# Softmax sums over the partitions in four 128x32 tiles of the array instead of 64x64 tiles, in three of four groups of an attention

## The chip, the cores and the metric

The kernel runs on one core of a Trainium2 chip, in f32 throughout. The metric is the device time of one launch in microseconds. All runs quoted were fast, at a granted TensorE clock of 0.992 to 0.995.

## The reference, cut to what matters

A group norm, a 1x1 convolution and two bottlenecks are run over 8 images of 512 channels and 32x32 positions. Each bottleneck has a 3x3 convolution and an attention of four heads of 64 channels over 1024 positions:

```python
        qkv = conv2d(x, qkv_w, 0).reshape(b, 3, HEADS, HD, hw)
        q, k, v = (qkv[:, 0], qkv[:, 1], qkv[:, 2])
        r = (rw + rh).reshape(1, HEADS, HD, hw)
        logits = jnp.einsum('bhdi,bhdj->bhij', q, k + r) * HD ** (-0.5)
        a = jax.nn.softmax(logits, axis=-1)
        out = jnp.einsum('bhij,bhdj->bhdi', a, v)
```

The change touches only how the denominators of the softmax are summed.

## The kernel before

An attention is run in four groups: a pair of heads (`c`) and a half of the 1024 queries (`half`). Keys lie on the partitions. TensorE makes the logits of 128 keys at a time, ScalarE takes exponentials into `pt`, VectorE adds these over the key blocks into `acc` (128 partitions x 2 heads x 512 queries), and TensorE multiplies `pt` with V. What is then left of the denominator is a sum over the 128 partitions of `acc`:

```python
            def sums(g):
                ps = ps_big.tile([P, 2, HALF], F32, tag="big", name="s_ps")
                acc = accs.pop(g)
                for kh in range(2):
                    r = slice(kh * HD, (kh + 1) * HD)
                    for hd in range(2):
                        nc.tensor.matmul(
                            ps[hd * HD : (hd + 1) * HD, kh, :], ones[r], acc[r, hd, :],
                            start=True, stop=True,
                        )
                s_dram = tc.dram_tile([2, 2, HALF], F32, name=f"s_dram{at + g}")
                rows = [act.tile([P, HALF], F32, tag=t, name="s_row", bufs=2) for t in ("h", "t")]
                for kh, row in enumerate(rows):
                    nc.scalar.copy(row, ps[:, kh, :])
                    for hd in range(2):
                        nc.sync.dma_start(s_dram[kh, hd : hd + 1, :], row[hd * HD : hd * HD + 1, :])
                return ps, rows, s_dram
```

The sums of both halves of the partitions go to memory, come back spread over the partitions, are added (`total`), inverted, written and read once more, copied to 64 partitions for each head (`spread`). Then VectorE scales the output with them (`scale`). The main loop places these steps:

```python
            for i in range(len(pairs) + 1):
                if i < len(pairs):
                    added = logits(pairs[i])
                    g, at_q = divmod(i, NQ)
                    with tc.issue_after(added.ins):
                        if at_q == NQ - 2 and g > 0:
                            rss[g - 1] = spread(g - 1, s_drams[g - 1])
                        if at_q == 0 and g > 1:
                            scale(g - 2, rss.pop(g - 2))
                if i > 0:
                    times_v(pairs[i - 1])     # the last pair of a group also empties av: ScalarE copy, VectorE add
                    g, j0 = pairs[i - 1][0]
                    if j0 == 0:
                        if g > 0:
                            s_drams[g - 1] = sums(g - 1)[2]
                        ...                   # work of other stages behind this group
```

The last group's sums stay in PSUM on all partitions and are inverted there; the change leaves that group as it was. `ps_av`, the accumulator for V, has one buffer, so the next group's product with V waits until VectorE has emptied it.

Of the kernel before, what the change touches and what calls it, by code (L numbers as in the profile page):

```python
# [40 lines left out]
F32 = mybir.dt.float32  # L41
# [7 lines left out]
P = 128  # L49
# [8 lines left out]
def kernel(  # L58
# [16 lines left out]
    nc = tc.nc  # L75
# [8 lines left out]
    HALF = 512  # L84
# [9 lines left out]
    act = fast.enter_context(tc.tile_pool(name="act", bufs=1))  # L94
# [77 lines left out]
    ones = const.tile([P, HD], F32, name="ones")  # L172
# [64 lines left out]
    QP = 2 * HALF // P  # L237
    sums_all = const.tile([P, NSUM, QP], F32, name="sums_all")
# [8 lines left out]
    def stages(act, small, ps_big, ps_av, n_pt):  # L247
# [207 lines left out]
        def attention_fast(n, z, at, behind):  # L455
# [5 lines left out]
            ao = act.tile([P, NM, HW], F32, tag="z", name="ao")  # L461
# [4 lines left out]
            pts, accs, avs = {}, {}, {}  # L466

            def logits(pair):
                g, j0 = pair[0]
                c, half = groups[g]  # L470
                pt = act.tile([P, PAIR, 2, HALF], F32, tag="pt", name="pt", bufs=n_pt)
                pts[pair[0]] = pt
                for i, (_, j) in enumerate(pair):
                    ps = ps_big.tile([P, 2, HALF], F32, tag="big", name="l_ps")
                    for hd in range(2):
                        r = slice(hd * HD, (hd + 1) * HD)
                        for kh in range(2):
                            o = j * P + kh * HD
                            nc.tensor.matmul(  # L479
                                ps[kh * HD : (kh + 1) * HD, hd, :], kr[r, c, o : o + HD],  # L480
                                q[r, c, ts(half, HALF)], start=True, stop=True,
                            )
                    exp = nc.scalar.activation(pt[:, i], ps, AF.Exp, scale=SCALE)  # L483
                if pair is pairs[-1]:
                    with tc.issue_after(exp.ins):
                        table_of(AF.Silu)
                if j0 == 0:
                    accs[g] = act.tile([P, 2, HALF], F32, tag="acc", name="acc", bufs=2)
                    return nc.vector.tensor_tensor(accs[g], pt[:, 0], pt[:, 1], ALU.add)  # L489
                for i in range(PAIR):  # L490
                    ins = nc.vector.tensor_tensor(accs[g], accs[g], pt[:, i], ALU.add)  # L491
                return ins

            def times_v(pair):
                g, j0 = pair[0]
                c, half = groups[g]
                pt = pts.pop(pair[0])
                if j0 == 0:
                    avs[g] = ps_av.tile([P, 2, HALF], F32, tag="av", name="av_ps")
                for i, (_, j) in enumerate(pair):  # L500
# [3 lines that stand above are left out]
                            o = c * P + hd * HD  # L504
                            nc.tensor.matmul(  # L505
                                avs[g][hd * HD : (hd + 1) * HD, kh, :], vT[r, j, o : o + HD],
                                pt[r, i, hd, :], start=(j == 0), stop=(j == NJ - 1),
                            )
                if j0 + PAIR == NJ:
                    av = avs.pop(g)  # L510
                    dst = ao[:, c, ts(half, HALF)]
                    nc.scalar.copy(dst, av[:, 0])
                    nc.vector.tensor_tensor(dst, av[:, 1], dst, ALU.add)  # L513

            def sums(g):

                ps = ps_big.tile([P, 2, HALF], F32, tag="big", name="s_ps")
                acc = accs.pop(g)
                for kh in range(2):
# [11 lines that stand above are left out]
                        nc.sync.dma_start(s_dram[kh, hd : hd + 1, :], row[hd * HD : hd * HD + 1, :])  # L531
                return ps, rows, s_dram

            def total(g, s_dram):

                cs = small.tile([P, 2, QP], F32, tag="cs", name="cs", bufs=2)
                nc.sync.dma_start(cs, s_dram.rearrange("k h (i r) -> (h i) k r", r=QP))
                nc.vector.tensor_tensor(sums_all[:, at + g, :], cs[:, 0], cs[:, 1], ALU.add)
                return sums_all[:, at + g, :]

            def spread(g, s_dram):

                rs = act.tile([P, HALF], F32, tag="rs", name="rs", bufs=2)
                rc = small.tile([P, QP], F32, tag="rc", name="rc", bufs=2)
                nc.vector.reciprocal(rc, total(g, s_dram))
                r_dram = tc.dram_tile([2, HALF], F32, name=f"r_dram{at + g}")
                nc.sync.dma_start(r_dram.rearrange("h (i r) -> (h i) r", r=QP), rc)
                for hd in range(2):
                    nc.sync.dma_start(
                        rs[hd * HD : (hd + 1) * HD, :], r_dram[hd : hd + 1, :].to_broadcast([HD, HALF])  # L550
                    )
                return rs

            def scale(g, rs):
                c, half = groups[g]
                dst = ao[:, c, ts(half, HALF)]
                nc.vector.tensor_tensor(dst, dst, rs, ALU.mult)
# [5 lines left out]
            s_drams, rss = {}, {}  # L563
# [10 lines that stand above are left out]
                    times_v(pairs[i - 1])  # L574
                    g, j0 = pairs[i - 1][0]
                    if j0 == 0:
                        if g > 0:
                            s_drams[g - 1] = sums(g - 1)[2]
                        with tc.issue_after(added.ins):
                            behind.get(g, lambda: None)()  # L580
            with tc.issue_after(added.ins):
                behind.get(len(groups), lambda: None)()

            g = len(groups) - 1
            ps, rows, s_dram = sums(g)
            with tc.issue_after(added.ins):
                behind.get(len(groups) + 1, lambda: None)()
            scale(g - 1, rss.pop(g - 1))
# [1 line left out]
            nc.vector.tensor_tensor(rs, ps[:, 1, :], rows[0], ALU.add)  # L590
            nc.vector.reciprocal(rs, rs)
            scale(g, rs)
            return ao, lambda: total(g, s_dram)

        def attention_general(n, z):
            IB = 256
# [169 lines left out]
    ps_big = fast.enter_context(tc.tile_pool(name="ps_big", bufs=3, space=PSUM))  # L766
# [34 lines left out]
    for b in range(B):  # L801
# [54 lines left out]
        ao, check = s.attention_fast(0, z, b * N * NM * NH, {**{g: ahead for g in range(NG)}, NG: first, NG + 1: second})  # L856
# [28 lines left out]
        ao, check = s.attention_fast(1, z, (b * N + 1) * NM * NH, {1: ahead, NG: first, NG + 1: second})  # L885
# [26 lines left out]
    with tc.If(held < P):  # L912
        with ExitStack() as gs:
# [6 lines left out]
            g = stages(g_act, g_small, g_big, g_av, 3)  # L920
            with tc.For_i(0, B, 1) as b:
# [6 lines left out]
                for n in range(N):  # L928
                    z = g.conv3x3(n, g.tiles_in(yi), lambda oc: [load_u(n, oc, i) for i in range(PAIRS)])
                    ao = g.attention_general(n, z)  # L930
# [57 lines left out]
```

## Time and profile before

| | before |
|---|---|
| median of 3 runs | 2502.18 us (2498.42 to 2503.01) |
| span of the profiled run | 2497.3 us |
| TensorE, VectorE, ScalarE busy | 97%, 60%, 39% |
| TensorE's share of the chain that ended last | 86% |

The profile's chain of waits starts at the last instruction and goes back to what released each one. A microsecond taken from an instruction on it shortens the run, until another path is the longest. Time off it costs nothing. The lines are in the prediction.

### The profile page before, as it was taken

How to read it: one execution, taken by the hardware profiler on the slowest of the kernel's cores; microseconds unless marked ns; L12 is line 12 of the kernel's file. 1: busy time of each engine (PE TensorE's matmuls, PEld its weight loads, DVE VectorE, ACT ScalarE, POOL GpSimd, SP SyncE). 2: the span in 40 equal slices, each digit the busy share in tenths (PEclk: the TensorE clock that was granted, in tenths of full speed). 3: DMA queues.
4: the chain of work that ended last, by engine and by line, in shares of the span. 5: the costliest groups of instructions: out<-in, count | busy, mean ns of one | idle time of the engine just before them, and what ended most of it. 6: DMA issues, size and time to landing. Idle time of an engine off the chain costs nothing.

```text
span 2497.3 us, 35914 instructions
## 1 busy us (share of the span) xinstructions
PE 2424.1 (97%) x14626; PEld 1208.3 (48%) x14626; DVE 1497.6 (60%) x2530; ACT 969.9 (39%) x1328; POOL 104.6 (4%) x355
## 2 busy tenths in 40 slices
PE   6789999999999999999999999999999999999998
PEld 4436446363463634636355363644536454363543
DVE  7678554766456664666546665566564665636654
ACT  2453522525135261443514434153441534326252
POOL 1000000000100001000010000100001000010001
PEclk9899999999999999999999999999999999999999
DMA  6124014040140402304032040402205021050202
GB/s 234 61 91 154 27 39 169 15 152 11 57 150 15 152 15 73 130 15 152 15 119 89 19 143 15 173 35 64 98 14 202 10 74 55 18 194 11 72 10 65
DMA packets 88348, 200.42 MB, mean 80 GB/s; under 512 B 34032, under 2 KB 43760, under 8 KB 75888
## 3 DMA queue, kind: packets, MB, share of 16 engines
q1 hardware_dynamic: 74224, 152.40, 17.7%
q0 software_dynamic: 11808, 45.62, 5.1%
q8 instruction: 117, 1.92, 0.3%
q14 instruction: 55, 0.45, 0.1%
q10 hardware_dynamic: 2144, 0.03, 0.0%
HBM read 167.94 MB, written 30.08 MB: 79 GB/s over the span
## 4 chain that ended last, share of the span: by engine, by line
PE 86%; DVE 5%; ACT 3%; issue 2%; DMA 1%; SPq 0%; ACTq 0%; DVEq 0%
PE ps L266 34%; PE av_ps L505 15%; PE l_ps L479 14%; PE c_ps L673 13%; PE v_ps L445 4%; PE m_ps L694 4%; ACT pt L483 2%; PE s_ps L522 2%; DVE ao L513 1%; DVE acc L489 1%; DMA rs<-r_dram 1%; ACT t L252 1%; DVE acc L491 1%; DMA r_dram<-rc 0%; DVE v_in L325 0%
## 5 line engine op out<-in xcount | busy, mean ns | idle before, releaser
L483 ACT ACTIVATE pt<-l_ps 128x1024 f32<-128x1024 f32 x512 | 495.5, 1025 | 195.6 <-PE l_ps L479 195.6
L491 DVE TENSOR_TENSOR acc<-acc,pt 128x1024 f32<-128x1024 f32 x384 | 469.0, 1221 | 128.3 <-ACT pt L483 102.8
L505 PE MATMUL av_ps<-pt,vT 64*64 64x512 f32 x4096 | 485.4, 591 | 16.6 <-DVE ao L513 14.4
L479 PE MATMUL l_ps<-q,kr 64*64 64x512 f32 x4096 | 485.7, 592 | 7.3 <-ACT pt L483 7.3
L673 PEld LDWEIGHTS c_ps<-v_in,u 128*128 128x128 f32 x2688 | 302.6, 192 | 11.2 <-issue 6.7
L673 PE MATMUL c_ps<-v_in,u 128*128 128x128 f32 x2688 | 303.2, 275 | 4.0 <-DVE v_in L325 4.0
L505 PEld LDWEIGHTS av_ps<-pt,vT 64*64 64x64 f32 x4096 | 152.8, 133 | 312.6 <-issue 221.6
L479 PEld LDWEIGHTS l_ps<-q,kr 64*64 64x64 f32 x4096 | 153.4, 133 | 287.1 <-issue 263.4
L266 PE MATMUL ps<-z,qkv_sb 128*128 128x512 f32 x512 | 229.3, 595 | 0.4
L266 PE MATMUL ps<-x,w 128*128 128x512 f32 x512 | 227.4, 601 | 2.2 <-DVE x L401 2.2
L266 PE MATMUL ps<-ypad,w 128*128 128x512 f32 x512 | 227.8, 594 | 0.5 <-ACT t L252 0.5
L266 PEld LDWEIGHTS ps<-x,w 128*128 128x128 f32 x512 | 97.0, 192 | 130.5 <-issue 124.6
L489 DVE TENSOR_TENSOR acc<-pt 128x1024 f32<-128x1024 f32 x64 | 78.4, 1225 | 135.5 <-ACT pt L483 135.5
L266 PEld LDWEIGHTS ps<-ypad,w 128*128 128x128 f32 x512 | 96.5, 190 | 126.0 <-issue 124.6
L433 DVE TENSOR_TENSOR kr<-ps,rw_sb 128x512 f32<-128x512 f32 x64 | 41.2, 686 | 186.0 <-PE ps L266 186.0
L252 ACT ACTIVATE t<-ps,bh,sh 128x512 f32<-128x512 f32 x58 | 42.7, 775 | 274.6 <-PE ps L266 168.0
L266 PEld LDWEIGHTS ps<-z,qkv_sb 128*128 128x128 f32 x512 | 94.7, 190 | 107.2 <-issue 91.8
L756 DVE TENSOR_TENSOR t<-t,x_res 128x512 f32<-128x512 f32 x64 | 44.0, 692 | 170.2 <-ACT t L252 141.9
L529 ACT COPY s_row<-s_ps 128x512 f32<-128x512 f32 x128 | 68.7, 589 | 152.0 <-PE s_ps L522 152.0
L266 PE MATMUL ps<-y,w 128*128 128x512 f32 x256 | 118.0, 599 | 3.7 <-ACT t L252 3.7
L332 ACT COPY m<-c_ps 128x256 f32<-128x256 f32 x96 | 35.5, 369 | 220.8 <-PE c_ps L673 214.6
L266 PE MATMUL ps<-ylast,w 128*128 128x512 f32 x256 | 117.2, 595 | 0.0
(118 smaller groups left out, 2102.1 us busy)
## 6 DMA issues: line engine op xcount, KB each, us to landing
u<-u SPq DMA_DIRECT2D x84, 1024.0 KB
w<-in_cv_w_dram SPq DMA_DIRECT2D x25, 1024.0 KB
x<-in_x_dram SPq DMA_DIRECT2D x32, 512.0 KB
x_res<-in_x_dram POOLq DMA_DIRECT2D x64, 256.0 KB, 3.7
out_dram<-t POOLq DMA_DIRECT2D x62, 256.0 KB, 2.7
u<-u_new POOLq DMA_DIRECT2D x12, 1024.0 KB, 5.4
rs<-r_dram SPq DMA_DIRECT2D x96, 128.0 KB
raw<-in_m_cv_w_dram SPq DMA_DIRECT2D x8, 576.0 KB
```

The costliest lines, as they stand in the source:

```text
L252: return nc.scalar.activation(dst, src, AF.Silu, scale=sh[:, k : k + 1], bias=bh[:, k : k + 1])
L266: nc.tensor.matmul(ps[:, half, :], w_of(k), rhs_of(k, half), start=(k == begin), stop=(k == end))
L445: nc.tensor.matmul(ps[:, at, :], z[:, k, ts(j0 + at, P)], qkv_sb[:, n, k, 2 * C : 3 * C], start=(k == 0), stop=(k == NM - 1),)
L479: nc.tensor.matmul(ps[kh * HD : (kh + 1) * HD, hd, :], kr[r, c, o : o + HD], q[r, c, ts(half, HALF)], start=True, stop=True,)
L483: exp = nc.scalar.activation(pt[:, i], ps, AF.Exp, scale=SCALE)
L489: return nc.vector.tensor_tensor(accs[g], pt[:, 0], pt[:, 1], ALU.add)
L491: ins = nc.vector.tensor_tensor(accs[g], accs[g], pt[:, i], ALU.add)
L505: nc.tensor.matmul(avs[g][hd * HD : (hd + 1) * HD, kh, :], vT[r, j, o : o + HD], pt[r, i, hd, :], start=(j == 0), stop=(j == NJ - 1),)
L522: nc.tensor.matmul(ps[hd * HD : (hd + 1) * HD, kh, :], ones[r], acc[r, hd, :], start=True, stop=True,)
L529: nc.scalar.copy(row, ps[:, kh, :])
L673: nc.tensor.matmul(ps[:, row, col, :], us[i][:, k, row, col, :], vs[i][:, k, row, col, :], start=(k == 0), stop=(k == NM - 1),)
L694: nc.tensor.matmul(pss[oc][:, half, :], m2_sb[:, n, k, ts(oc, P)], ao[:, k, ts(half, HALF)], start=(k == 0), stop=(k == NM - 1),)
```

## The change

The intent: 128x32 tiles sum over all 128 partitions at once, one tile for each head and half of the group's queries. So each instruction has 256 columns, not 512, and there is no second half to add. The way in which TensorE's array is split, here into four tiles of 64x64 or four of 128x32, is called its mode below; the logits and the products with V stay in 64x64 tiles. ScalarE copies one 128x256 tile, one transfer takes four rows away, and the way back lands where the reciprocal reads.

```diff
             def sums(g):
+                NQ4 = HALF // 2
+                ps = ps_big.tile([P, NQ4], F32, tag="big", name="s_ps")
+                acc = accs.pop(g)
+                for at_q in range(4):
+                    hd, part = divmod(at_q, 2)
+                    nc.tensor.matmul(
+                        ps[at_q * 32 : (at_q + 1) * 32, :], ones[:, 0:32], acc[:, hd, ts(part, NQ4)],
+                        start=True, stop=True, tile_position=(0, at_q * 32),
+                    )
+                s_dram = tc.dram_tile([4, NQ4], F32, name=f"s_dram{at + g}")
+                row = act.tile([P, NQ4], F32, tag="h", name="s_row", bufs=2)
+                nc.scalar.copy(row, ps)
+                nc.sync.dma_start(s_dram, row[0:P:32, :])
+                return s_dram
+
+            def last_sums(g):
... (the sums as before, for the last group)
-            def total(g, s_dram):
-
+            def last_total(g, s_dram):
                 cs = small.tile([P, 2, QP], F32, tag="cs", name="cs", bufs=2)
                 nc.sync.dma_start(cs, s_dram.rearrange("k h (i r) -> (h i) k r", r=QP))
                 nc.vector.tensor_tensor(sums_all[:, at + g, :], cs[:, 0], cs[:, 1], ALU.add)
+
+            def total(g, s_dram):
+
+                nc.sync.dma_start(sums_all[:, at + g, :], s_dram.rearrange("a (i r) -> (a i) r", r=QP))
                 return sums_all[:, at + g, :]
... (the calls renamed)
```

More of the change, by code (lines that the diff above doesn't have):

```diff
@@ L577, in attention_fast @@
                         if g > 0:
-                            s_drams[g - 1] = sums(g - 1)[2]
+                            s_drams[g - 1] = sums(g - 1)
                         with tc.issue_after(added.ins):
@@ L584, in attention_fast @@
             g = len(groups) - 1
-            ps, rows, s_dram = sums(g)
+            ps, rows, s_dram = last_sums(g)
             with tc.issue_after(added.ins):
@@ L592, in attention_fast @@
             scale(g, rs)
-            return ao, lambda: total(g, s_dram)
+            return ao, lambda: last_total(g, s_dram)
         def attention_general(n, z):
```

## The prediction

> **What bounds the kernel now.** I read the page first: the busy shares, then its chain that ended last, then the costliest groups.
>
> ```profile
> PE 2424.1 (97%) x14626; PEld 1208.3 (48%) x14626; DVE 1497.6 (60%) x2530; ACT 969.9 (39%) x1328; POOL 104.6 (4%) x355
> ...
> PE 86%; DVE 5%; ACT 3%; issue 2%; DMA 1%; SPq 0%; ACTq 0%; DVEq 0%
> ...
> L529 ACT COPY s_row<-s_ps 128x512 f32<-128x512 f32 x128 | 68.7, 589 | 152.0 <-PE s_ps L522 152.0
> ...
> L332 ACT COPY m<-c_ps 128x256 f32<-128x256 f32 x96 | 35.5, 369 | 220.8 <-PE c_ps L673 214.6
> ```
>
> TensorE is the bound: it is busy 97% of the span, and 86% of the chain of work that ended last lies on it. VectorE (60%) and ScalarE (39%) have slack on average, so work taken from them counts only at the places where the chain passes through them. The ScalarE copies of the sums' rows, L529, run 128 times, twice for each of the 64 groups (8 images x 2 bottlenecks x 4 groups).
>
> Next I went through the whole chain, stretch by stretch. The piece of the sums (s_ps) is on it 62 times out of 64: 44 times at 0.86 us and twice at 0.90 us in the groups that the change touches, and 16 times at 1.02 us in each attention's last group, which it doesn't touch. So 46 of the 48 changed groups have their sums on the path, and TensorE time gained or lost there counts nearly in full. This stretch of the chain has two group boundaries of one attention (columns: start us, duration us, what, count):
>
> ```profile
> 897.86 1.72 PE av_ps L505 x16
> 899.58 0.90 PE l_ps L479 x8
> 900.48 0.02 issue
> 900.50 1.95 ACT pt L483 x2
> ...
> 904.22 0.70 DVE ao L513
> 904.91 0.04 issue
> 904.96 1.95 PE av_ps L505 x16
> 906.90 0.90 PE s_ps L522 x8
> ...
> 908.31 0.59 ACT s_row L529
> 908.90 0.94 ACT pt L483
> ...
> 912.86 2.25 DMA r_dram<-rc
> ...
> 915.62 3.98 DMA rs<-r_dram
> ```
>
> The first boundary is the usual kind: TensorE's next product with V waits until VectorE has emptied its one accumulator (L513), which stands behind the group's first two exponentials. The wait is short: logits start at 899.58, three stages of 1.72 us would end at 904.74, and the product starts at 904.96. The second is the rarer kind: the sums' copies delay the exponentials, these the adds, and then the reciprocal's way through memory ends last. DMA pieces "rs" stand only four times on the whole chain.
>
> **What the Trainium skill says.** Three places bear on this.
> - "TensorEngine Tiling (Array Packing)", Key Properties: "Changing tiling mode (not just tile) drains the TensorE". The trace agrees and gives the price, because this kernel changes between 64x64 tiles and the whole array elsewhere. The first line here is undisturbed, from another attention, the others are a stretch with changes:
>
> ```profile
> 727.46 6.87 PE ps L266 x16
> ...
> 932.43 7.06 PE ps L266 x16
> 939.49 1.02 PE s_ps L522 x8
> 940.51 3.63 PE ps L266 x8
> ```
>
>  Sixteen whole-array matmuls take 6.87 us, but 7.06 us right after tiled ones: 0.19 us for the change. The sums take 1.02 us in place of 0.86 when whole-array matmuls precede them: 0.16 us for a change the other way. After the small group-norm matmul the logits take 1.88 us instead of 1.72, again 0.16.
> - "TensorE: Matmul & The Clock Gate", Measured speedup vs the span model: three column tiles of 32 columns gave 2.38 times the speed of one after another. No 128x32 tile runs in the kernel before, so the trace cannot confirm it for this shape. For 64x64 tiles it shows full overlap: one set of four instructions starts every 0.43 us, the time of one whole-array matmul of 512 columns (6.87 us / 16).
> - "PSUM — Partial Sum Buffer", PSUM bank collisions raise a hardware error: different column tiles may write one bank at the same time, on disjoint partitions. So four 128x32 tiles may share one bank; nothing in the trace before shows that shape.
>
> **The change part by part.** The order of TensorE's instructions is the same before and after but for the sums themselves; I compared the two built programs.
>
> *Sums on TensorE, removed.* An f32 matmul is two instructions here (512 instructions for 64 groups of four matmuls), so a group's sums are eight instructions of 512 columns in 64x64 tiles: two sets of four, 2 x 0.43 = 0.86 us, with no change of mode, since logits and products with V use 64x64 tiles too.
>
> *Sums on TensorE, added.* Eight instructions of 256 columns in 128x32 tiles. The contraction is now over all 128 partitions at once, so no second half is left to add. If four overlap as before, a set takes half as long: the V projection of 256 columns takes 6.04 us for 28, 0.216 each, against 0.429 at 512. Two sets: 0.43 us, 0.43 saved. But the mode changes twice, into 128x32 and back: 0.16 + 0.19 = 0.35 us, if a change between two tiled modes costs what one to the whole array does. I assume that; it is the largest term not measured. Net: 0.86 - 0.43 - 0.35 = 0.08 us a group.
>
> *Where the mode changes anyway.* In 14 groups (two in each of the seven first-bottleneck attentions that prepare another image) a group-norm matmul on the whole array follows the sums directly. There only one change of about 0.17 us is added: 0.86 - 0.43 - 0.17 = 0.26 us. Sum: 14 x 0.26 + 34 x 0.08 = 6.4 us; with two groups off the path about **6 us**.
>
> *ScalarE.* Two copies of 128x512 (1.07 us together in the timeline, where they overlap a little) become one of 128x256, 0.37 us by L332's row. That is 0.7 us a group, 34 us in all, but in the usual boundary ScalarE waits 1.4 us for TensorE soon after the copies, so nothing comes of it. It counts at the rarer kind.
>
> *VectorE.* The add of the two halves goes (128x8, 163 ns and some 30 ns of gap, 48 times). It, too, is on the path only in the rarer kind.
>
> *DMA.* Four row transfers become one of four rows, each issue taking 0.25 us on its queue; the way back is one transfer still, landing directly where the reciprocal reads it. At the rarer kind of boundary the gain is 0.7 + 0.2 = 0.9 us, times four is 3.6; but once the reciprocals come in time the usual wait remains, so I count **3 us**.
>
> Total: about 9 us, 0.4%. From the median of 2502 this gives 2493; for a possibly cheaper change of mode I move it to **2491 us**.
>
> **The rivals.**
> 1. *The change of mode is free or hidden between tiled modes.* Then 0.43 us x 46 is 20 us, with the other 3 us some 2479. For: both modes are tiled and need fewer columns to run out. Against: the skill says any change of mode drains, and the trace has a price of 0.16 to 0.19 at all that I looked at.
> 2. *The drain eats more than the gain.* If each change costs 0.3 us, a group costs 1.03 in place of 0.86: 46 x 0.17 = 8 us longer, near 2507 with the 3 us of the other terms. For: loads of the stationary operand run ahead of the matmuls now and cannot across a change, and in four narrow tiles these come in short sets. Against: the measured changes already contain this.
> 3. *128x32 tiles do not overlap for f32.* Eight times 0.216 is 1.73 us, with the changes 2.08: 1.2 us longer x 46 = 56 us, about 2555, slower by 2.2%. For: every tile now streams all 128 rows with its own data, twice the row streams of 64x64. Against: the skill's speedup for three column tiles. Two at a time would give 1.2 us a group, 16 us longer.
> 4. *The relief of ScalarE and VectorE is worth more.* If the buffer of the sums were what logits wait for, 34 us of ScalarE work might count. Against: ScalarE's own waits before exponentials are 195.6 us, all for TensorE's logits, and TensorE waited for exponentials before logits only 7.3 us in all.
>
> **Range and chances.** The mode term spans about -20 to +8 us, and the shorter way of the reciprocals 0 to -5; repeats of the kernel before differ by 5 us. Eight times in ten this is 2472 to 2507. Faster by 2% would need 50 us, more than all the sums in the changed groups cost (46 x 0.86 = 40 us): 0.01. Slower by 2% needs rival 3: 0.03. The rest, 0.96, is within 2%.
>
> **What would show it.** In the chain after, the changed sums' piece should last about 0.43 us plus 0.16 for entering, and the logits after it 1.9 instead of 1.72. If the piece is 0.43 and the logits stay at 1.72, rival 1 holds; if the sums' instructions start one after another 0.2 us apart, rival 3. ScalarE's row copies should be 48 at 0.37 us and 32 at 0.59. The waits of the scaling (L557's counterpart) for "rs", 44.9 us in 21 cases now, should shrink, and "rs" should nearly leave the chain. The prediction would be wrong if the chain at the group boundaries moved to something that I took as slack, such as a transfer that lands later because its four rows lie on four partitions only.

## The result, and the profile after

| | before | after |
|---|---|---|
| median (6 runs each) | 2502.60 us | 2486.82 us |
| lowest to highest | 2498.42 to 2504.68 | 2486.56 to 2488.19 |
| span of the profiled run | 2497.3 us | 2485.1 us |
| ratio of fast runs | | 0.994 (0.9927 to 0.9953) |

A ratio is the mean time of one kernel's fast runs over that of the other's of the same rounds, so it is not quite the ratio of the medians. Executions in which one die ran at a lower clock are left out of the means. The change gained about 15 us, 0.6%, which is clear of the noise but far under the 2% that counts as a change of speed here; the result is right. Note the ranges too: repeats before spread over 6 us, after over 1.6.

These lines of the page of the kernel after, and of its list of groups, answer to those of before (busy time; chain by engine; groups with count, busy us, mean ns):

```profile
PE 2416.4 (97%) x14626; PEld 1198.2 (48%) x14626; DVE 1488.6 (60%) x2482; ACT 939.7 (38%) x1280; POOL 104.9 (4%) x355
...
PE 86%; DVE 5%; ACT 3%; issue 2%; DMA 0%; POOL 0%; SPq 0%; ACTq 0%; DVEq 0%
...
L523 PE MATMUL s_ps<-acc,ones 128*32 128x256 f32 x384 | 30.7, 391 | 0.0
L529 ACT COPY s_row<-s_ps 128x256 f32<-128x256 f32 x48 | 17.9, 372 | 71.5 <-PE s_ps L523 71.5
L548 ACT COPY s_row<-s_ps 128x512 f32<-128x512 f32 x32 | 17.2, 591 | 60.0 <-PE s_ps L541 60.0
```

TensorE runs as many instructions as before, 384 of them narrow. ScalarE lost 30 us of work, VectorE 9 us. DMA has left the chain's rounded shares. The chain through the same attention as in the prediction, after:

```profile
884.64 1.72 PE av_ps L505 x16
886.36 0.57 PE s_ps L523 x8
886.93 1.88 PE l_ps L479 x16
...
893.96 0.90 PE l_ps L479 x8
894.86 0.02 issue
894.88 1.95 ACT pt L483 x2
...
898.60 0.70 DVE ao L513
899.29 0.04 issue
899.34 1.95 PE av_ps L505 x16
901.28 0.57 PE s_ps L523 x8
901.85 1.88 PE l_ps L479 x16
...
908.88 0.90 PE l_ps L479 x8
909.78 0.02 issue
909.81 1.95 ACT pt L483 x2
```

The sums last 0.57 us, and the logits after them 1.88 in place of 1.72, 0.16 longer. So the sums now cost 0.57 + 0.16 = 0.73 us, where they cost 0.86 before. Both boundaries are now of the usual kind; the copies of the sums and the transfers of the reciprocals are gone from this stretch.

To see where the whole difference lies, I took the start of every matmul from the traces and measured each attention from its first logits to the first matmul after it. The first attention, which shares VectorE with one-off work on the filters, stands apart. "Late" is what a group boundary waited beyond the regular stall of 0.41 us that 30 boundaries of the other 15 attentions have in both kernels.

| us | before | after | difference |
|---|---|---|---|
| 15 attentions | 888.3 | 877.2 | -11.1 |
| of it: late at boundaries | 3.8 | 0.4 | -3.4 |
| first attention | 75.1 | 72.7 | -2.4 |
| everything else of the span | 1533.9 | 1535.1 | +1.2 |

An attention of the second bottleneck without any late wait takes 58.59 us before and 58.20 after, 0.39 = 3 x 0.13. One of the first bottleneck takes 59.54 and 58.83, 0.71 = 0.13 + 2 x 0.29, because the group-norm matmuls follow two of its sums. So TensorE's part is 9 x 0.39 + 6 x 0.71 = 7.8 us of the 11.1; with the first attention it should be 8.5 (an estimate: the first attention's sums are not told apart there). The rest is late waits. The two traces differ by 12.2 us, the medians by 15.8: the profiled run of before is a fast one, 2498.8 us. The other 3 to 4 us lie in executions without a trace, so what they consist of is not shown.

### The profile page after: what moved, and what is told of

It reads as the page before. It is cut to its first block, busy times and chain, and to the rows that moved or that the text cites. A ratio compares the mean times of both kernels' runs of the same rounds, so it can differ in the third digit from the quotient of the medians.

```text
span 2485.1 us, 35553 instructions
## 1 busy us (share of the span) xinstructions
PE 2416.4 (97%) x14626; PEld 1198.2 (48%) x14626; DVE 1488.6 (60%) x2482; ACT 939.7 (38%) x1280; POOL 104.9 (4%) x355
## 4 chain that ended last, share of the span: by engine, by line
PE 86%; DVE 5%; ACT 3%; issue 2%; DMA 0%; POOL 0%; SPq 0%; ACTq 0%; DVEq 0%
PE ps L266 33%; PE av_ps L505 15%; PE l_ps L479 14%; PE c_ps L695 13%; PE v_ps L445 4%; PE m_ps L716 4%; ACT pt L483 3%; PE s_ps L523 1%; DVE ao L513 1%; PE s_ps L541 1%; ACT t L252 1%; DVE acc L491 0%; DVE acc L489 0%; DVE v_in L325 0%; DVE st L368 0%
## 5 line engine op out<-in xcount | busy, mean ns | idle before, releaser
L445 PE MATMUL v_ps<-qkv_sb,z 128*128 128x256 f32 x512 | 115.7, 379 | 0.0
```

The source lines that it names most:

```text
L445: nc.tensor.matmul(ps[:, at, :], z[:, k, ts(j0 + at, P)], qkv_sb[:, n, k, 2 * C : 3 * C], start=(k == 0), stop=(k == NM - 1),)
```

## The experiments

My theory had two terms: TensorE spends 8.5 us less on the sums, and the shorter way of the reciprocals takes away late waits. The first rival: it is all TensorE's, and the rest is chance. Further questions were what the mode changes cost and whether the four tiles overlap. All were timed in five rounds against the kernel before.

### The changed kernel again

> The changed kernel as it is, on the same chip as the next three, to compare them with. Expected 15 to 16 us under the kernel before (2487 against 2502), with a spread of repeats under 2 us, where the kernel before spreads over 6 us.

2487.29 us (2486.13 to 2487.55), before 2501.72 (2498.03 to 2504.94); ratio 0.9941 (0.9928 to 0.9955). That is 14.4 us, just under the 15 to 16 expected; the spread of 1.4 us is as expected.

### TensorE's part alone, first try

```diff
-                        ps[at_q * 32 : (at_q + 1) * 32, :], ones[:, 0:32], acc[:, hd, ts(part, NQ4)],
+                        ps[at_q * 32 : (at_q + 1) * 32, :], halves, acc[:, hd, ts(part, NQ4)],    # halves = 0.5
...
+                for kh, row in enumerate(rows):          # two copies to 128x512, as before
+                    nc.scalar.copy(row.rearrange("p (a q) -> p a q", a=2), ps.unsqueeze(1).to_broadcast([P, 2, NQ4]))
+                    for hd in range(2):
+                        nc.sync.dma_start(s_dram[kh, hd].rearrange("(a q) -> a q", a=2), row[hd * HD : (hd + 1) * HD : 32, 0:NQ4])
```

> Only TensorE's part of the change: sums in four 128x32 tiles, but ScalarE copies two rows of 128x512, four transfers, the way back through a small tile and the add on VectorE stay as before (the stationary operand is 0.5, so that the doubled halves add up to the right sums). Theory (two terms: TensorE 8.5 us by the traces, the rest a shorter way of the reciprocals): about 8.5 us under before, and the repeats spread as widely as before's (some 5 us), because the reciprocals still come late now and then. Rival (all of the gain is TensorE's): 15 us under before.

2501.24 us (2500.27 to 2504.58): ratio 1.0002 (0.9988 to 1.0015), no gain at all, where I expected 8.5 us. The result was right. This looked as if the narrow tiles brought nothing. But the trace said otherwise: the sums had shrunk on TensorE as in the changed kernel, and late waits in the 15 attentions had grown from 3.8 to 10.9 us. The list of waits (who, for what: us in total, times, longest) showed why; first the kernel before, then this one:

```profile
DVE sums_all L538 <- DMA cs<-s_dram: 4.1, 4, 1.8
```

```profile
DVE sums_all L565 <- DMA cs<-s_dram: 34.8, 35, 2.7
```

My stand-in for the old row transfers was slower than the original. Each transfer read two partitions instead of one, the four took 2.0 us to issue and not 1.1, and the return of the sums began 4.5 us after the sums' start instead of 3.9, though the sums were done sooner. The run doesn't measure TensorE's part. It does show that these transfers are close enough to the path that some 0.7 us more go with the loss of all the gain.

### TensorE's part alone, with the transfers as they were

The edit is shown against the first try; the constant in `halves` is 1e6 here, so the result is wrong.

```diff
-                        nc.sync.dma_start(s_dram[kh, hd].rearrange("(a q) -> a q", a=2), row[hd * HD : (hd + 1) * HD : 32, 0:NQ4])
+                        nc.sync.dma_start(s_dram[kh, hd : hd + 1, :], row[hd * HD : hd * HD + 1, :])
```

> A second, cleaner try at TensorE's part alone. In the first one the four row transfers read two partitions each, their issue took 2.0 us where it takes 1.1 in the kernel before, and VectorE waited for the sums' return 35 times, not 4. Here each transfer reads one partition and 512 columns as before (the sums are wrong for half the queries on purpose, with a large constant). Theory (the mechanism has two terms; TensorE's 8.5 us is partly lost in waits for the reciprocals, as long as their way is the old one): 3 to 8 us under before, spread 4 us or more. Rival (TensorE's part brings nothing without the other): equal to before within 2 us.

2492.19 us (2490.98 to 2494.63), before 2501.94 (2498.7 to 2504.9); ratio 0.9961 (0.9948 to 0.9973). It is 9.8 us faster (6.8 to 13 by the interval), a little more than the 3 to 8 expected, with a spread of 3.7 us where 4 or more was expected. In the trace, the 15 attentions take 881.1 us, 7.2 less than before, and late waits remain at 4.3 us. So TensorE's part stands by itself, leaves the late waits, and is less than the whole gain.

### The rows' part alone

```diff
-                    nc.tensor.matmul(                     # four 128x32 tiles
+                    # 64x64 tiles, 512 columns, as before; a large constant as stationary operand
+                        nc.tensor.matmul(ps[hd * HD : (hd + 1) * HD, kh, 0:512], many[r], acc[r, hd, 0:512], ...)
-                nc.scalar.copy(row, ps)
+                nc.scalar.copy(row, ps[:, 0, 0:NQ4])
```

> Only the other part: the sums' matmuls stay in 64x64 tiles with 512 columns, but one copy of 128x256, one transfer of four rows, straight into the place the reciprocal reads. The sums are wrong on purpose (half the keys, some queries' sums twice, a large constant as the stationary operand), so the result is wrong and only the time counts. Theory: about 7 us under before, repeats within 2 us of each other, no transfer of reciprocals on the chain but in the first attention. Rival (all TensorE's): equal to before.

2496.66 us (2495.36 to 2501.43): ratio 0.9982 (0.9968 to 0.9996), 5.1 us faster by the medians (1 to 8 by the interval), where 7 was expected. In the trace, late waits in the 15 attentions are down from 3.8 to 0.55 us and these take 885.1 us, 3.2 less; pieces for the reciprocals stand on the chain in the first attention alone, as expected: the mechanism is there. In the 48 changed groups the return of the sums begins, by the median, 3.85 us after their first matmul in the kernel before, 3.44 with TensorE's part alone, 3.13 with the rows' part alone and 2.73 with both. The spread was not as expected: two of the five runs took 2501 us. The profiled one is one of these, and its excess is not in the boundaries but in the first attention (78.0 us) and in the first convolution (39.25 us). That stage takes 37.6 us in seven of the 14 traces and 39.25 in the other seven, this one among them, whatever the kernel; where it takes longer, it also starts sooner, so that it ends only 1.1 us later here than in the kernel before. I had no trace of a fast repeat to compare.

The two parts alone gain 9.8 and 5.1 us, 14.9 in sum; together they gained 14.4 in the repeat and 15.8 in the first comparison. The rival "all TensorE's" falls, by the narrow interval here and by the late waits in the traces. The parts add up within the noise, which is some 3 us for each; the two were measured on different chips, each against before.

### No change of mode

```diff
+                    # 64x64 tiles with 256 columns: the streaming time of the narrow tiles, no change of mode
+                        nc.tensor.matmul(ps[hd * HD : (hd + 1) * HD, kh, 0:256], many[r], acc[r, hd, 0:256], ...)
```

> The changed kernel without the change of tile mode: 64x64 tiles with 256 columns (wrong sums on purpose as in the run before), so the streaming time of the sums is that of the changed kernel and only the two mode changes are gone. Theory (a round trip costs 0.30 us in the trace after, 0.14 where a group-norm matmul follows): 34 x 0.30 + 14 x 0.14 = 12 us under the changed kernel, about 2475. Rival (the mode changes are hidden or the narrow tiles cost something else): equal to the changed kernel.

2478.76 us (2477.72 to 2480.34), 8.5 us under the changed kernel of the same rounds, not 12. In the attentions without group norm the theory holds to the last digit, 58.20 becoming 57.31 us, 0.89 = 3 x 0.30; those with it gain 0.57 where theory has 0.58, or less where they have late waits. The 15 take 866.4 us, 10.7 less than in the repeat of the changed kernel. The chain of this run, where the sums take 0.43 us and the logits after them are not longer:

```profile
888.46 0.43 PE s_ps L526 x8
888.89 1.72 PE l_ps L481 x16
```

What is missing in the profiled run, the slowest of the four, lies in the first attention, which took 76.3 us in place of 72.6. So a round trip between 64x64 and 128x32 costs 0.30 us, and the narrow tiles otherwise stream as fast as theory has it. How much of the 0.30 is a drain of the array and how much the first loads of the stationary operand in the new mode, the runs don't tell apart.

### All four matmuls in one tile

```diff
-                        ps[at_q * 32 : (at_q + 1) * 32, :], ones[:, 0:32], acc[:, hd, ts(part, NQ4)],
-                        start=True, stop=True, tile_position=(0, at_q * 32),
+                        ps, ones[:, 0:32], acc[:, hd, ts(part, NQ4)],          # ps has 32 partitions
+                        start=True, stop=True, tile_position=(0, 0),
... (the copy and the transfer take 32 and 4 neighbouring partitions)
```

> The changed kernel with all four matmuls of a group in the same 128x32 tile, at column 0, so that nothing can overlap (wrong sums on purpose: all four write one place). Theory (the four tiles overlap fully): eight times 0.213 us in place of two, 1.28 us more x 48 = 61 us over the changed kernel, near 2548. Rival (the tiles overlapped only in part, or not): less, down to equal.

2551.58 us (2548.17 to 2553.35), ratio to before 1.0194 (1.018 to 1.0207): 64 us over the changed kernel. It was run at another time. By starts of matmuls, sums take 62.3 us more in all, 1.28 in 47 of the 48 groups and 2.41 in one: eight instructions start one after another, 0.24 us apart at first and then mostly 0.216, where in four tiles the second set of four starts 0.24 us after the first. Four 128x32 tiles of f32 overlap fully.

### Two tiles

```diff
-                        ps[at_q * 32 : (at_q + 1) * 32, :], ones[:, 0:32], acc[:, hd, ts(part, NQ4)],
+                        ps[hd * HD : (hd + 1) * HD, :], ones, acc[:, hd, :],
-                        start=True, stop=True, tile_position=(0, at_q * 32),
+                        start=True, stop=True, tile_position=(0, hd * HD),
... (two matmuls for a group, one for each head; one copy of 128x512, one transfer of two rows)
```

> Right sums in two 128x64 tiles, one for each head with all 512 queries: four instructions of 512 columns, 0.86 us as in the kernel before, but with the mode changes; copies of one 128x512 row tile, one transfer. Theory: 0.43 us x 48 = 21 us over the changed kernel, near 2507; against the kernel before the mode changes cost about 12 us and the shorter way of the reciprocals brings some 7: about 5 us slower. Rival (it is the sum over all partitions at once that pays, not the fewer columns): as fast as the changed kernel.

2510.17 us (2509.5 to 2511.01), ratio 1.0032 (1.0018 to 1.0045), with a right result: 8 us slower than before, 23 slower than the changed kernel. It was run at another time. Expected were 5 and some 21. In its chain the sums have the old length plus the mode change, and this has the same size with half as many instructions:

```profile
896.23 1.01 PE s_ps L521 x4
897.24 1.88 PE l_ps L479 x16
```

Summing over all partitions at once doesn't pay by itself. It is the halved columns that pay for the mode changes.

### Scaling later, before and after

The late waits stand at one place: VectorE's scaling waits for the reciprocals, and the emptying of the accumulator for V stands behind it in VectorE's order. One edit moves the scaling behind that emptying:

```diff
-                        if at_q == 0 and g > 1:
+                        if at_q == 1 and g > 1:
                             scale(g - 2, rss.pop(g - 2))
```

> The kernel before with one edit: VectorE scales a group's output one pair of steps later, behind the emptying of the accumulator for V, not ahead of it. The reciprocals then have some 3.4 us more time and no longer stand before that emptying. Theory: the late reciprocals' stalls (about 7 us) go and with them the regular stall of 0.41 us at 30 boundaries (12 us): 19 us under before, near 2483, repeats within 2 us. Rival (the reciprocals' way was not what the change shortened): under 12 us gained.

> The changed kernel with the same edit. Theory: only the regular stall is left to take, 12 us under the changed kernel, near 2474. With the waits for reciprocals out of both, the difference between this run and the last is TensorE's term alone, 8.5 us. Rival (all of the gain is TensorE's): the difference stays at 15 us.

In the kernel before the edit gained 24.5 us: 2477.45 (2477.23 to 2477.78), ratio 0.9901 (0.9886 to 0.9916). In the changed kernel it came to 2474.56 (2473.28 to 2475.55), ratio 0.9888 (0.9873 to 0.9903), some 12.7 under the changed kernel. It was run at another time. Both results are right. The expected 19 us for the first were too few. In its trace the 15 attentions take 870.7 us, 17.6 less: the regular stalls of 30 boundaries (12.3 us, and 1.5 for the restarts) and all late waits (3.8) are gone. The chain runs through a boundary on TensorE alone:

```profile
887.70 1.72 PE l_ps L479 x16
889.42 1.72 PE av_ps L505 x16
891.14 1.72 PE l_ps L479 x16
892.85 1.72 PE av_ps L505 x16
894.57 1.72 PE l_ps L479 x16
896.29 1.72 PE av_ps L505 x16
898.00 0.86 PE s_ps L522 x8
```

The first attention gave 3.9 us more. The sum is 21.5; the profiled run of before was at the low end of its range, so a typical one may have had some 3 us more of late waits (an estimate, from its 2498.8 against the median of 2502; no trace shows it). And the spread: before 6.2 us, with the edit 0.55. So the waits for the reciprocals are the likely reason why the repeats of the kernel before differ. It can't be the only one: the run with the rows' part alone spread over 6 us with hardly a late wait in its trace.

The gap between the two edited kernels was 2.9 us. Theory wanted 8.5, the rival 15, and neither had it. I ran both again.

> The kernel before with the later scaling once more, on the same chip as the next two. Expected as measured: 2477.5 within 1 us.

> The changed kernel with the later scaling once more, to see whether its gap of 2.9 us to the one before it holds. By the trace, TensorE's term is 7.8 us in 15 of the 16 attentions, 2.0 are lost again to waits behind the group-norm matmuls, the first attention is 1.4 longer and the start of the first convolution, which the change doesn't touch, was 1.7 longer. If the last was chance: 3 to 5 us under the run before it. If the gap is TensorE's whole term after all: 8.5 us.

2478.88 us (2478.55 to 2479.46), 0.4 us outside the "within 1 us" expected, and 2474.66 (2474.55 to 2475.39), a gap of 4.2 us. The traces account for it. The attentions without group norm differ by 0.39 us, 57.67 to 57.28, as in the pair without the edit. Those with group norm differ by 0.39 as well, 58.62 to 58.23, and not by 0.71. Two lists of waits of the first pair (those of the second have the same numbers), for the kernel before with the edit and then for the changed one with it, name the cause:

```profile
PEld l_ps L479 <- DVE gr L387: 3.6, 7, 0.5
PEld l_ps L479 <- DVE gm L377: 3.4, 7, 0.5
```

```profile
PEld l_ps L479 <- DVE gr L387: 5.7, 7, 0.8
PEld l_ps L479 <- DVE gm L377: 5.7, 7, 0.8
```

The logits there wait for VectorE to read the small group-norm result out of PSUM, and with the sums shorter they arrive at this wait sooner. About half of what TensorE had gained at these places is lost again, 0.16 us of 0.29. So the 15 attentions differ by 5.8 us, and the first attention is 1.2 us longer in the changed kernel: 4.6 us in sum, near the 4.2 measured. In the first pair the changed kernel's profiled run also had the slow start of the first convolution, 39.25 us against 37.59; in the second pair the other one had it, 39.26 against 37.57. That stage is untouched, and as each kernel shows both values, I take this as chance.

### A version that should beat both

With the scaling late there is time to take the sums of the first two groups together, one trip into the narrow tiles less in each attention:

```diff
+            together = {2: (0, 1), 3: (2,)}
-                        if g > 0:
-                            s_drams[g - 1] = sums(g - 1)
+                        if g in together:
+                            s_drams[g] = sums(together[g])     # one copy, one transfer for both groups
... (spread and scale take the groups of a trip; the accumulated exponentials get a third buffer)
```

> A version that should beat both kernels: later scaling, and the sums of the first two groups of an attention taken together behind the third group's first pair (one more buffer for the accumulated exponentials), so that there is one trip into the narrow tiles and back less in each attention. Theory: a round trip costs 0.30 us, 16 x 0.30 = 4.8 us under late_after_2, near 2470; right result. Rival (another wait takes its place, such as the longer copy of the sums or four row transfers behind each other): equal to late_after_2.

2473.68 us (2470.84 to 2474.28), ratio 0.9883 (0.9868 to 0.9898), right result: 1.0 us under the later scaling alone, not 4.8. It is the fastest version I ran, by little. The attentions without group norm gained 0.29 us each as planned (57.28 to 56.99), but those with it became longer, 58.23 to 58.38. Its list of waits:

```profile
PEld l_ps L479 <- DVE gr L387: 9.9, 7, 1.4
PE l_ps L479 <- DVE gr L387: 3.7, 7, 0.5
```

The wait behind the second group-norm matmul grew. The first attention took 1.0 us longer in this trace, too (73.45 against 72.45). Two scalings now stand together on VectorE near it; that these delay the reading is argued from VectorE's order, not tested.

## Why the prediction was right

It said 2491 us in a range of 2472 to 2507, and "within 2%". Measured were 2486.82 us and 0.6%. The range was 35 us wide, and the working came to "about 9 us" where 15 were gained: both terms had the right sign and were too small. Of the 11 us forecast, 2 were a guess, "for a possibly cheaper change of mode"; that the changes then came out cheaper by just that (34 x 0.05 + 14 x 0.03 = 2.1 us) was luck.

- **The bound and the path.** Right. TensorE's sums lie on the path, and TensorE's saving alone passed into the time (9.8 us in the second try of TensorE's part).
- **Overlap and streaming.** Right: two sets of four in 0.43 us, shown by the run in one tile (1.28 us more for a group).
- **The mode changes.** The mechanism was right, the size a little too large. I took 0.35 us from changes between tiles and the whole array, and 0.17 where one was added. By starts of matmuls, entering costs 0.11, leaving 0.14 and 0.05, 0.30 for the round trip; where a group-norm matmul follows, the added part is 0.14. A plain group gained 0.13 and not 0.08, the others 0.29 and not 0.26. The sum "14 x 0.26 + 34 x 0.08 = 6.4 us" should have been 14 x 0.29 + 34 x 0.13 = 8.5.
- **The rarer kind of boundary.** The mechanism was right again, and the term probably too small: "I count 3 us" against 5.1 us for the rows' part alone, whose interval of 1 to 8 holds the 3 as well; the two traces give 3.4 us in 15 attentions. I had counted four cases in one trace; that execution was among the fastest of the kernel before, and the slower ones may have had more of these waits, which no trace shows. The usual wait was misread: "904.74" against 904.96 makes it 0.22 us, but 899.58 is where the chain's piece begins, not where the logits start. By starts of matmuls these began at 899.40, and the wait is 0.41 us. No term of the sum rests on it.
- **What would show it.** The chain's piece of 0.57 us followed by logits of 1.88, and 48 copies of 0.37 us beside 32 of 0.59, came as written; "rs" went from four pieces on the chain to one. The forecast that the waits for "rs" would shrink in total was wrong: they grew from 44.9 us in 21 cases to 57.8 in 17. Sixteen of these 17 are at the end of an attention, once in each, where VectorE waits and no matmul does. I should have split the row by place before using its total.
- **The rivals.** A free mode change would have made "some 2479"; the run without any came to 2478.76, though partly by chance, as the first attention took back 3.7 us of it. Tiles that don't overlap would have made some 2552, close to the "about 2555" of the prediction.

Left open: the first attention takes between 71.2 and 78.0 us over these kernels (80.0 in the run in one tile, where its sums alone are 5.0 us longer), and moves by several us when something small changes. One-off filter work shares VectorE and ScalarE with it, and the order of that work differs between the kernels; which instruction matters was not tested. It hid part of the expected gain of the run without mode changes.

## What to carry to other kernels

Before moving a small matmul to narrower tiles, weigh the columns saved against the round trip between modes, and look whether a neighbour already changes the mode: here the change paid more than twice as much beside a whole-array matmul. A wide spread of repeats is a reason to suspect a wait that varies from run to run, which a single trace can undercount. Look at what stands behind a waiting instruction in its engine's order: moving one scaling by one step was worth 23 to 25 us, more than the change itself. And a gain on the path can be lost at the next wait: with the scaling late, TensorE's 8.5 us came to 2.9 and 4.2.

## What the Trainium skill lacked or had wrong

- "TensorEngine Tiling (Array Packing)", Key Properties, says that a change of mode drains the TensorE but gives no time. Here a round trip from 64x64 to 128x32 tiles and back cost 0.30 us.
- "TensorE: Matmul & The Clock Gate", Measured speedup vs the span model, has three column tiles (2.38 times), not four, and names no type. Here eight instructions of 256 columns came in two sets, 0.24 us apart, in four 128x32 tiles of f32; in one tile they came one after another, mostly 0.216 us apart, and a group took 1.28 us more.
- The same page, The mechanism, says that loads of the stationary operand overlap with running matmuls only when the row group differs. Read alone, that does not fit: 16 whole-array matmuls of 512 columns took 6.87 us, 0.429 each, and 256 columns took 0.216 each, so loads of 0.19 us between them were hidden though all use all rows. The same section's remark on a background buffer for weights does fit.
- "DMA: Bandwidth & Descriptors": I found no time of issue by a transfer's shape there. Here four transfers of one partition and 512 columns took 1.1 us to issue, four of two partitions and 256 columns each took 2.0 us, and the changed kernel's one of four partitions and 256 columns 0.52.
